# Second attention layer: turned probabilities by sixteen SBUF-to-SBUF transfers a tile in place of a way through DRAM

## The chip, the cores and the metric

The kernel runs on one core of a Trainium2 chip, in fp32 (the attention mask is added in bf16). The metric is the device time of one execution in microseconds (us). Five engines work side by side: PE (TensorE, matmuls; PEld is its loading of weights), DVE (VectorE), ACT (ScalarE), POOL (GpSimd) and SP (SyncE). In this kernel SP does nothing but issue DMAs. Sixteen DMA engines move the data.

## The reference

x has the shape [8, 512, 512] (8 batches of 512 tokens), ctx [8, 120, 512] (120 keys a batch). Four sublayers are added to x one after the other, each on a layer norm of x:

```python
x = x + tanh(g_xattn[0]) * L0_xattn(layernorm(x), ctx, ctx, Wq, Wk, Wv, Wo)
x = x + tanh(g_ffn[0])   * L0_ffn(layernorm(x), Wc, bc, W1, b1, W2, b2)
x = x + tanh(g_xattn[1]) * L1_xattn(layernorm(x), ctx, ctx, key_mask, Wq, bq, Wk, bk, Wv, bv, Wo, bo)
x = x + tanh(g_ffn[1])   * L1_ffn(layernorm(x), W_r, W_k, W_v, mu_r, mu_k)

# attention, both layers (mask and biases in the second alone); H = 16 heads of 32
q, k, v = split_heads(Q @ Wq.T), split_heads(K @ Wk.T), split_heads(V @ Wv.T)
scores = einsum('bhqd,bhkd->bhqk', q, k) / sqrt(32)
probs = softmax(scores)                         # [8, 16, 512, 120]
out = einsum('bhqk,bhkd->bhqd', probs, v) @ Wo.T
```

The change is in the second attention layer. The product of the probabilities with v sums over the keys, so PE needs the probabilities with keys on the partitions, while the softmax leaves them with tokens on the partitions: they have to be turned. L1_ffn is called ChannelMix in the kernel; it mixes each token with the one before it and multiplies with three 512 x 512 weights (W_k, W_r, W_v).

## The kernel before

x stays in SBUF, as 32 tiles of 128 tokens (NT = 32), 4 tiles a batch (TB = 4). The stages follow one another: attention 1 (0 to some 420 us in the profile), routed FFN (to 625), attention 2 (628 to 1040), ChannelMix (to the end). The order of the work is written out by hand: the instructions of each engine run in the order of the program (`tc.manual_schedule`), and waits between engines are semaphores.

**A step of the attention.** `steady(k)` (the last function below) works on four tiles at once, for k from 4 to 27:
- scores of tile k on PE (L656 adds the mask, L666 multiplies: 32 matmuls), into PSUM in two halves; a half comes free when tile k's exponentials have read it;
- softmax of tile k: the maximum of each half on DVE (L710, `nmx`), 32 exponentials on ACT with their sums (L721), 1/sum on DVE (L727) and the division on POOL (L731), in two halves u = 1 and u = 0;
- the turn of tile k's second half and tile k-1's first half on DVE (L793);
- the output product of tile k-3 (L878) and its addition to x (L888);
- products for the next batch's queries (L165, seven products for four tiles, by the scheme of seven in place of eight; three of four steps hold two products, the step with k % 4 = 3 holds one);
- the transposing of normalized x of tile k+8 (L588), the product of probabilities and v of tile k-2 (`attend`, L861), and the normalization of tile k+9.

**How probabilities are turned.** For the 22 tiles in `CROSSED` (4 to 25 of each layer) PE isn't used for it. The softmax writes a tile's probabilities as [128 tokens, 16 heads, 4 x 32 places], where key 4f + k stands at place f of piece k; 30 of 32 places hold keys and two hold zeros. DVE transposes blocks of 32 x 32 in place (L793). Then the 32 keys of a block are on partitions, but of four token groups q on four groups of partitions. Two DMAs a tile write the tile to a plane in DRAM (L796, 512 KB for each half), and four DMAs read it back (L806, 240 KB each), for piece k the 30 rows of each token group, to every fourth partition of `prT`:

```python
# turn_blocks, L796                       # fetch_blocks, L806
plane[:, :, u, :] <- pr half u            prT[k:120:4] <- plane[k, :30]     # for k in 0..3
```

In `steady(k)` the plane's last half (tile k-1, u = 0) is written near the start, behind the maxima; the fetch of tile k-1 is issued at the end, behind `attend(k-2)`, because `prT` has one buffer. `attend(k-1)` reads it at the end of `steady(k+1)`. All DMAs of this stage are issued by SP. The probabilities themselves (`pr`) have two buffers in the pool `soft`; the zeros in each are written once, and for the crossed tiles the same two buffers are handed on (the list `wide`).

`self.turned` (L236) is true in the second layer alone.

**ChannelMix beside it.** In the second layer `self.then` is a method of ChannelMix, which starts its own first work within the attention. `start` (L1396 and on) is called in the first slots: it takes the pool `cm_w` and loads `mu` (8 DMAs, L1406) and the weights wk and wr (4 DMAs of 256 KB each, L1415). wk is first read by POOL at 992.84 us (L91), wr near 1043 us, both in ChannelMix's preparations.

Of the kernel before, what the change touches and what calls it, by code (L numbers as in the profile page):

```python
# [9 lines left out]
FP = mybir.dt.float32  # L10
# [7 lines left out]
P = 128  # L18
B, S, D = 8, 512, 512
LK = 120  # L20
NH, HD = 16, 32
NT = B * S // P
TB = S // P
NC = D // P
# [8 lines left out]
KB, KF = 4, 30  # L33
CROSSED = range(TB, NT - TB - 2)
# [186 lines left out]
class CrossAttention:  # L221
# [455 lines left out]
    def softmax(self, t, sv):  # L677

        nc, soft = self.nc, self.soft
        if t - 2 in CROSSED and t in CROSSED:
            whole = self.wide.pop(0)
        else:
            whole = soft.tile([P, NC * S], FP, name="pr")
            if t in CROSSED:
                rows = whole.rearrange("p (n f) -> p n f", f=32)  # L690
                nc.gpsimd.memset(rows[:, :, KF:], 0.0)
        if t in CROSSED:
            self.wide.append(whole)
        sm = soft.tile([P, 2, 2, NC], FP, name="sm")
        rs = soft.tile([P, 2, 2, NC], FP, name="rs")
        nmx = [soft.tile([P, 2, NC, 1], FP, name=f"nmx{u}") for u in range(2)]
        self.probs[t] = whole
        crossed = t in CROSSED
        if crossed:
            half = [  # L700
                whole[:, u * 1024 : (u + 1) * 1024].rearrange(
                    "p (k h f) -> p k h f", k=KB, h=2 * NC
                )[:, :, :, :KF]
                for u in range(2)
            ]
        else:
            half = whole[:, : NH * LK].rearrange("p (u h k) -> p u h k", u=2, k=LK)

        def largest(u):
            nc.vector.tensor_reduce(nmx[u], sv[u], AX.X, ALU.max, negate=True)  # L710

        def exponentials(u, heads=range(2 * NC)):
            for h in heads:
                j, hc = divmod(h, NC)
                src = sv[u][:, j, hc, :]
                if crossed:
                    dst = half[u][:, :, h, :].rearrange("p k f -> p f k")
                    src = src.rearrange("p (f k) -> p f k", k=KB)
                else:
                    dst = half[:, u, h, :]  # L720
                nc.scalar.activation(  # L721
                    dst, src, AF.Exp, bias=nmx[u][:, j, hc, :],
                    accum_out=sm[:, u, j, hc : hc + 1],
                )

        def divide(u):
            nc.vector.reciprocal(rs[:, u], sm[:, u])  # L727
            by = rs[:, u].rearrange("p j h -> p (j h)")
            if crossed:
                by = by.unsqueeze(1).unsqueeze(3).to_broadcast([P, KB, 2 * NC, KF])  # L730
                nc.gpsimd.tensor_tensor(half[u], half[u], by, ALU.mult)  # L731
            else:
                by = by.unsqueeze(2).to_broadcast([P, 2 * NC, LK])
                nc.gpsimd.tensor_tensor(half[:, u], half[:, u], by, ALU.mult)

        return largest, exponentials, divide
# [52 lines left out]
    def turn_blocks(self, t, u):  # L789

        nc = self.nc
        pr = self.probs[t][:, u * 1024 : (u + 1) * 1024]
        nc.vector.transpose(pr, pr)  # L793
        if u == 1:
            self.planes[t] = self.dram.tile([KB, P, 2, 256], FP, name="plane")
        nc.sync.dma_start(  # L796
            out=self.planes[t][:, :, u, :].rearrange("k p e -> p k e"),
            in_=pr.rearrange("p (k e) -> p k e", k=KB),
        )

    def fetch_blocks(self, t):

# [125 lines left out]
    def steady(self, k):  # L928

        b, f = divmod(k + TB, TB)  # L930
        crossed = k in CROSSED
        if k == TB:
            self.transpose_probs_late(k - 1)
        largest, exponentials, divide = self.softmax(k, self.score_products(k))
        for u in (1, 0):
            largest(u)
        if k - 1 in CROSSED:
            self.turn_blocks(k - 1, 0)
        done = {TB: TB - 2, TB + 1: None}.get(k, k - 3)
        if done is not None:  # L940
            self.output(done, range(2 if done == TB - 1 else 0, NC))
        exponentials(1)
        divide(1)
        if done is not None:
            self.after(done, "final")
        exponentials(0, range(4))
        if f == 0:
            self.begin_queries(b)
        self.q7.postponed = True
        self.q7.next()  # L950
        exponentials(0, range(4, 8))
        if crossed:
            self.turn_blocks(k, 1)
        self.q7.settle(1)
        divide(0)
        if f != TB - 1:
            self.q7.next()
        if f == 0:
            self.sum_tokens(2)
        self.q7.settle()  # L960
        self.after(k, "route")
        if k + 8 < NT:
            self.transpose_x(k + 8)
        if k == TB:
            self.attend(k - 1)
        elif k == TB + 1:
            self.output(TB - 1, range(2))
        else:
            self.attend(k - 2)
        if k - 1 in CROSSED:  # L970
            self.fetch_blocks(k - 1)
        if k + 9 < NT:
            self.normalize(k + 9)
        if done is not None:
            self.after(done, "late")
# [403 lines left out]
class ChannelMix:  # L1379
# [16 lines left out]
    def start(self):  # L1396
        nc = self.nc
        wr_in, wk_in, wv_in, mu_in = self.ins
        self.pool = pool = self.es.enter_context(
            self.tc.tile_pool(name="cm_w", bufs=1, side="right", reuse_waits="tile")  # L1400
        )
        self.mu = pool.tile([P, 2, NC], FP, name="mu")
        for m in range(2):
            by_row = mu_in[:, m, :].rearrange("(j e) q -> q e j", j=NC)
            for q in range(4):
                nc.sync.dma_start(out=self.mu[32 * q : 32 * q + 32, m, :], in_=by_row[q])  # L1406
        self.om = pool.tile([P, 2, NC], FP, name="om")
        self.wk = self.load_rows(pool.tile([P, NC, D], FP, name="wk"), wk_in)
        self.wr = self.load_rows(pool.tile([P, NC, D], FP, name="wr"), wr_in)

    def load_rows(self, w, w_in):

# [33 lines left out]
    def in_slot(self, s, attention, stage):  # L1446

        nc = self.nc
        self.at = attention
        if stage == 2 and s >= 1:  # L1450
            attention.stats(s - 1)
        if stage == "final" and s < NT - 2 * TB:
            attention.stats(s, False)
        if stage == "late" and s < NT - 2 * TB:
            attention.scales(s)
        if s == -1:
            self.start()
        if stage == "head" and s == NT:
            self.sum_value_weights()
            self.k7.next()  # L1460
        if stage == "end" and s < NT:
            self.normalize(s - NT + 2 * TB)
        if stage == "end" and s == NT + 1:
            for c in range(NC):
                self.mix_chunk(0, 0, c)
            self.k7.next()
        if stage == "end" and s == NT + 2:
            for step in self.sum_steps(0, 0):
                step()
            self.k7.next(2)  # L1470
            self.sum_gate_weights()
        if stage != "route":
            return
        if s == TB + 1:
            nc.vector.tensor_scalar(self.om, self.mu, -1.0, 1.0, ALU.mult, ALU.add)
        i = s - (NT - 9)
        if 0 <= i - 1 < TB:
            self.transpose(i - 1)
        if 0 <= i < TB:
            xn = self.at.norm.tile([P, D], FP, name="xn")  # L1480
            self.normalize(i, xn)
        if s == NT - 4:
            wv = self.at.pool.tile([P, NC, D], FP, name="wv", tag="wq")
            self.wv = self.load(wv, self.ins[2])
            self.weight_sums = self.sum_key_weights()
        if 0 <= s - (NT - 5) < NC:
            self.mix_chunk(0, 1, s - (NT - 5))
        if s in (NT - 4, NT - 3):
            for _ in range(2):
                self.weight_sums.pop(0)()  # L1490
        if s == NT - 2:
            self.key_sums = self.sum_steps(0, 1, nc.gpsimd)
        if s in (NT - 2, NT - 1):
            for _ in range(2):
                self.key_sums.pop(0)()
        if s == NT - 1:
            self.k7 = self.keys(0)
            self.k7.next()
        if s in (NT, NT + 1):
            self.k7.next()  # L1500
# [385 lines left out]
```

## Time and profile before

| | |
|---|---|
| median of three runs | 1345.24 us (1342.72, 1345.24, 1347.89) |
| the profiled execution | 1344.26 us, its span 1342.4 us |
| granted PE clock | 0.996 |
| PE busy | 1283.4 us, 96% of the span |
| DVE, ACT, POOL busy | 75%, 59%, 53% |
| DMA queue of SP | 173.43 MB, 41.3% of 16 engines |
| plane written (L796) | 88 DMAs of 512 KB, landing 3.4 us after issue |
| prT fetched (L806) | 176 DMAs of 240 KB, landing 4.1 us after issue |

The profiled execution lies 1.0 us under the median and 1.9 us above its own span. A row of a group gives the line, engine, operation, tiles (out<-in) and count; in a row of a line's DMAs, the three numbers are minimum, median and maximum of one issue in ns. "SPq" is SP's issuing of DMAs, which the profile doesn't count as busy time. A timeline row gives start, duration, engine, line and operation, and in brackets the idle time ahead of it and what ended it. A wait for several semaphores is put down to the one that came last by the profile.

### The profile page before, as it was taken

What the parts mean: (1) busy time and instruction counts of PE and PEld (TensorE: products, weight loads), DVE (VectorE), ACT (ScalarE), POOL (GpSimd) and SP (SyncE); (2) the same over time, 40 slices, a digit from 0 to 9 for tenths busy, and PEclk for the clock granted to TensorE, in tenths of its full rate; (3) what the DMA queues carried; (4) which work ended last, traced back from release to release, by engine and by line L of the source; (5) the groups of instructions that cost most, each with busy time, mean ns of one, the idle gap of its engine ahead of it and who ended that gap; (6) DMA issues with size and microseconds to landing.
All of it is one profiled execution on the core that took longest, in us unless ns stands there. A gap on an engine that the chain in (4) does not pass through costs nothing. (4 is left out here: it accounts for less than half of the span.)

```text
span 1342.4 us, 32798 instructions
## 1 busy us (share of the span) xinstructions
PE 1283.4 (96%) x13072; PEld 1014.9 (76%) x13072; DVE 1001.5 (75%) x1476; ACT 791.4 (59%) x2512; POOL 705.2 (53%) x626
## 2 busy tenths in 40 slices
PE   7999999999999988999999989999999999999997
PEld 6886777777776877888888767676766888878886
DVE  5877776777685676777888687777775977878876
ACT  1368788888774445455226778888874454444442
POOL 4855655565542002555797777777665234434333
PEclk9999999999999999999999999999999999999999
DMA  9501766666603256431402067767621211333201
GB/s 308 194 1 62 225 208 205 222 211 214 195 26 110 75 168 212 127 112 63 155 12 54 32 205 222 216 211 226 213 81 33 63 67 60 94 94 94 63 32 63
DMA packets 136382, 175.53 MB, mean 131 GB/s; under 512 B 9197, under 2 KB 88557, under 8 KB 136229
## 3 DMA queue, kind: packets, MB, share of 16 engines
q1 hardware_dynamic: 136229, 173.43, 41.3%
q8 instruction: 103, 1.69, 0.5%
q14 instruction: 50, 0.41, 0.1%
HBM read 101.18 MB, written 72.22 MB: 129 GB/s over the span
## 5 line engine op out<-in xcount | busy, mean ns | idle before, releaser
L721 ACT ACTIVATE pr<-s,nmx 128x120 f32<-128x120 f32 x768 | 273.5, 497 | 43.1 <-DVE nmx L710 24.8
L878 PE MATMUL ops<-wo,aT 128*128 128x512 f32 x512 | 237.0, 604 | 3.6 <-ACT aT L869 2.2
L731 POOL TENSOR_TENSOR pr<-pr,rs 128x960 f32<-128x960 f32 x88 | 160.2, 1820 | 139.0 <-DVE rs L727 137.2
L721 ACT ACTIVATION_READ_ACCUMULATOR pr<-s,nmx 128x1 f32 x768 | 195.0, 254 | 0.0
L878 PEld LDWEIGHTS ops<-wo,aT 128*128 128x128 f32 x512 | 91.9, 189 | 99.8 <-issue 89.1
L1353 POOL TENSOR_TENSOR r<-r,b 128x1024 f32<-128x1024 f32 x31 | 73.5, 2377 | 147.8 <-ACT r L1352 147.8
L710 DVE TENSOR_REDUCE nmx<-s 128x8 f32<-128x960 f32 x96 | 106.7, 1153 | 56.9 <-PE s L666 56.8
L793 DVE STREAM_TRANSPOSE pr<-pr 128x1024 f32<-128x1024 f32 x88 | 109.1, 1240 | 37.3 <-POOL pr L731 37.3
L165 PE MATMUL qps<-xnT,wq 128*128 128x256 f32 x512 | 119.0, 380 | 0.0
L165 PEld LDWEIGHTS qps<-xnT,wq 128*128 128x128 f32 x512 | 96.3, 189 | 23.3 <-issue 10.3
L52 DVE BATCH_NORM_STATS2 bnst<-x 128x6 f32<-128x512 f32 x128 | 87.6, 684 | 0.4
L1629 ACT ACTIVATE kT<-kT 128x512 f32<-128x512 f32 x32 | 19.9, 622 | 108.1 <-DVE kT L183 59.6
L759 POOL TENSOR_TENSOR pr<-pr,rs 128x960 f32<-128x960 f32 x32 | 58.1, 1823 | 40.8 <-DVE rs L758 31.5
L861 PE MATMUL aps<-prT,v 120*32 120x128 f32 x2048 | 69.2, 276 | 7.7 <-DVE qT L212 3.3
L888 DVE SCALAR_TENSOR_TENSOR x<-ops,gates,x 128x512 f32<-128x512 f32 x64 | 47.7, 746 | 34.6 <-PE ops L878 34.1
L666 PE MATMUL s<-kT,qT 32*128 32x120 f32 x2048 | 71.6, 275 | 0.0
L666 PEld LDWEIGHTS s<-kT,qT 32*128 32x128 f32 x2048 | 65.7, 186 | 7.0 <-issue 4.9
L861 PEld LDWEIGHTS aps<-prT,v 120*32 120x32 f32 x2048 | 52.2, 109 | 21.3 <-issue 8.6
L1352 ACT COPY r<-rps 128x1024 f32<-128x1024 f32 x31 | 31.4, 1013 | 59.1 <-PE rps L1340 59.1
L1340 PE MATMUL rps<-ident,rT 128*128 128x128 f32 x512 | 61.9, 275 | 2.1 <-DVE rT L1320 1.8
L1350 DVE TENSOR_TENSOR r<-rps,b 128x1024 f32<-128x1024 f32 x33 | 40.4, 1225 | 28.3 <-PE rps L1340 28.3
L1340 PEld LDWEIGHTS rps<-ident,rT 128*128 128x128 f32 x512 | 55.5, 141 | 7.7 <-issue 4.8
(240 smaller groups left out, 3092.1 us busy)
## 6 DMA issues: line engine op xcount, KB each, us to landing
plane<-pr SPq DMA_DIRECT2D x88, 512.0 KB, 3.4
prT<-plane SPq DMA_DIRECT2D x176, 240.0 KB, 4.1
w<-in_w_dram SPq DMA_DIRECT2D x32, 512.0 KB, 4.4
x<-in_x_dram SPq DMA_DIRECT2D x8, 1024.0 KB, 16.8
aside<-x SPq DMA_DIRECT2D x32, 256.0 KB, 3.0
x<-aside SPq DMA_DIRECT2D x8, 1024.0 KB, 10.2
rows<-xn SPq DMA_DIRECT2D x14, 512.0 KB, 2.8
xn<-rows SPq DMA_DIRECT2D x56, 128.0 KB, 3.2
```

Of the source, the lines that this page charges most:

```text
L52: cm.nc.vector.bn_stats(st, cm.x[:, t, :])
L165: self.nc.tensor.matmul(ps[:, m, :], rows[:, k, m * n : (m + 1) * n], columns[:, k, :], start=(k == 0), stop=(k == 1),)
L666: nc.tensor.matmul(s[j // 2][:, j % 2, hc * LK : (hc + 1) * LK], self.qT[b][r : r + 32, hc, toks], self.kT[r : r + 32, hc, keys], start=no ...
L710: nc.vector.tensor_reduce(nmx[u], sv[u], AX.X, ALU.max, negate=True)
L721: nc.scalar.activation(dst, src, AF.Exp, bias=nmx[u][:, j, hc, :], accum_out=sm[:, u, j, hc : hc + 1],)
L731: nc.gpsimd.tensor_tensor(half[u], half[u], by, ALU.mult)
L759: nc.gpsimd.tensor_tensor(pr[:, js, :, :], pr[:, js, :, :], rs[:, js, :, :].to_broadcast([P, 2, NC, LK]), ALU.mult,)
L793: nc.vector.transpose(pr, pr)
L861: nc.tensor.matmul(out, self.v[b // 2][:LK, b % 2, h * HD : (h + 1) * HD], p, start=True, stop=True,)
L878: nc.tensor.matmul(ops, self.aT[t][:, c, :], self.wo[:, c, :], start=(c == 0), stop=(c == NC - 1),)
L1340: nc.tensor.transpose(ps[:, k // 4, (k % 4) * P : (k % 4 + 1) * P], self.rT[:, 16 * tq + 8 * h + k, :], self.cm.ident,)
L1353: nc.gpsimd.tensor_tensor(r, r, b2, ALU.add)
```

## The change

In the second layer only:
- the probabilities of a tile are laid out piece by piece, "(k u e)" in place of "(u k e)": the 512 values of piece k lie side by side on a partition, and a half u is four pieces of 256 (`half_of`);
- the plane in DRAM goes. `move_blocks(k-1)`, called in `steady(k)` right behind `turn_blocks(k-1, 0)`, issues 16 DMAs from SP, for each token group q and piece k one: 32 partitions x 512 values (64 KB), from 32 neighbouring partitions of `pr` to every fourth partition of `prT`;
- `prT` gets a second buffer for odd tiles ("prT2", in the place of ChannelMix's wr) and `pr` a third one ("pr2", in the place of wk, first used by tile 4);
- the loads of wk and wr move from ChannelMix's start to the steps s = 26 and s = 30 of the attention (NT - 6, NT - 2).

The order of PE's and ACT's instructions stays. On DVE the 44 transposes of the layer read and write 128 x 4 x 256 in place of 128 x 1024, on POOL its divisions get one more dimension and one memset of zeros is added. SP issues 352 DMAs for the 22 tiles, where it issued 132.

```diff
@@ softmax
-        if t - 2 in CROSSED and t in CROSSED:
+        bufs = 3 if self.turned else 2
+        if t - bufs in CROSSED and t in CROSSED:
             whole = self.wide.pop(0)
         else:
-            whole = soft.tile([P, NC * S], FP, name="pr")
+            if self.turned and t == CROSSED[0]:
+                whole = self.then.__self__.place("pr2", "wk")
+            else:
+                whole = soft.tile([P, NC * S], FP, name="pr")
...
             half = [
-                whole[:, u * 1024 : (u + 1) * 1024].rearrange(
-                    "p (k h f) -> p k h f", k=KB, h=2 * NC
-                )[:, :, :, :KF]
+                self.half_of(whole, u).rearrange("p k (h f) -> p k h f", h=2 * NC)[:, :, :, :KF]
                 for u in range(2)
             ]
@@ turn_blocks
-        pr = self.probs[t][:, u * 1024 : (u + 1) * 1024]
+        pr = self.half_of(self.probs[t], u)
         nc.vector.transpose(pr, pr)
+        if self.turned:
+            return
...
+    def half_of(self, whole, u):
+        if self.turned:
+            halves = whole.rearrange("p (k u e) -> p u k e", k=KB, u=2)
+        else:
+            halves = whole.rearrange("p (u k e) -> p u k e", k=KB, u=2)
+        return halves[:, u]
+
+    def move_blocks(self, t):
+        if t % 2:
+            prT = self.then.__self__.place("prT2", "wr")
+            prT = prT.rearrange("p (q e) -> p q e", q=4)
+        else:
+            prT = self.late.tile([P, 4, 512], FP, name="prT", bufs=1)
+        blocks = self.probs.pop(t).rearrange("p (k e) -> p k e", k=KB)
+        for q in range(4):
+            for k in range(KB):
+                self.nc.sync.dma_start(
+                    out=prT[k::KB, q], in_=blocks[32 * q : 32 * q + 32, k]
+                )
+        self.probs[t] = prT
@@ steady
         if k - 1 in CROSSED:
             self.turn_blocks(k - 1, 0)
+            if self.turned:
+                self.move_blocks(k - 1)
...
-        if k - 1 in CROSSED:
+        if k - 1 in CROSSED and not self.turned:
             self.fetch_blocks(k - 1)
@@ ChannelMix.start
-        self.wk = self.load_rows(pool.tile([P, NC, D], FP, name="wk"), wk_in)
-        self.wr = self.load_rows(pool.tile([P, NC, D], FP, name="wr"), wr_in)
+
+    def place(self, name, tag):
+        return self.pool.tile([P, NC * S], FP, name=name, tag=tag)
@@ ChannelMix, called by the attention at each step s
+        if s == NT - 6:
+            wk = self.pool.tile([P, NC, D], FP, name="wk")
+            self.wk = self.load_rows(wk, self.ins[1])
+        if s == NT - 2:
+            wr = self.pool.tile([P, NC, D], FP, name="wr")
+            self.wr = self.load_rows(wr, self.ins[0])
```

More of the change, by code (lines that the diff above doesn't have):

```diff
@@ L797, in turn_blocks @@
             out=self.planes[t][:, :, u, :].rearrange("k p e -> p k e"),
-            in_=pr.rearrange("p (k e) -> p k e", k=KB),
+            in_=pr,
         )
+    def half_of(self, whole, u):
[17 more added lines that the diff above has]
+        self.probs[t] = prT
     def fetch_blocks(self, t):
```

## The prediction

> **What bounds the kernel now.** I read the page first (which engine is busy where), then a table by stretches of the second layer's steady part, then what TensorE waited for there, then single waits in the timeline, and last the rows of the DMAs by line. The table by stretches of the steady part (us; then busy time and instructions of PE, PEld, DVE, ACT, POOL; clock; DMA share; GB/s):
>
> ```profile
> 780.00:860.00 80.00, 77.44 (x825) 54.27 (x823) 60.95 (x92) 66.24 (x307) 60.55 (x47) 1.00 0.73 219
> 860.00:940.00 80.00, 79.51 (x774) 54.75 (x768) 61.83 (x90) 65.58 (x307) 60.24 (x52) 1.00 0.72 219
> 940.00:980.00 40.00, 38.56 (x387) 26.80 (x389) 27.07 (x41) 32.86 (x158) 24.60 (x20) 1.00 0.71 218
> ```
>
> PE is busy for 195.5 of 200 us: the stage runs at PE's pace, and the DMA engines, at 0.71 to 0.73, wait for nobody else. All that is left to win is in the other 4.5 us. The waits of PE between 780 and 980, and the three places where prT stands behind them:
>
> ```profile
> PE aps L861 <- DMA prT<-plane: 2.5, 2, 1.6
> PE aps L861 <- PE xnps L588: 1.5, 4, 0.8
> PE ops L878 <- ACT aT L869: 0.4, 1, 0.4
> ...
> 782.19 1.08 PE L861 MATMUL aps<-prT,v 120*32 120x128 f32 x32 [1.56 <-DMA prT<-plane]
> ...
> 866.19 1.08 PE L861 MATMUL aps<-prT,v 120*32 120x128 f32 x32 [0.28 <-PE xnps L588]
> ...
> 979.94 1.08 PE L861 MATMUL aps<-prT,v 120*32 120x128 f32 x32 [0.93 <-DMA prT<-plane]
> ```
>
> The reader is to see that the turned probabilities are late for a few tiles only. The second kind of line names PE itself, which had long been done; the last prT transfer landed 0.13 to 0.23 us ahead of each of these starts, and 0.5 to 1.6 us ahead in all other tiles. So prT stands behind 2.5 + 1.5 = 4.0 us, and no more than that can be won.
>
> **What the change takes out.** For 22 tiles the plane in DRAM goes, with 2 + 4 transfers a tile. Of the 4.0 us not all comes back, because the next scores wait for PSUM that ACT's exponentials free, and these end shortly before. Tile by tile, that slack (next scores' start less the end of the last exponential) is 0.35 us behind 782.19, 0.60 behind 791.09, and -0.1 to 0.0 in the four short slots (828, 866, 904, 941), which PE enters after some 8.3 us in place of 9.73. At 979.94, DVE's next maximum has 0.2 us. That gives about 0.5 + 0.75 + 4 x 0.1 + 0.2 = **-1.9 us**, if the new transfers are in time. The third buffer of probabilities gains nothing by itself: the exponentials start 0.22 to 0.24 us after the maximum (nmx) that they read, so no buffer held them.
>
> **What it adds.** 16 transfers a tile from SP's queue, 352 in all, where 132 were. Each carries 32 rows of 2 KB, from 32 neighbouring partitions to every fourth partition of prT. They are issued one after the other from the moment of the first half's turn (now the plane write, 769.55 for tile 4 and 966.97 for tile 25). The whole question is what one issue costs SP. These are the rows (duration of an issue, ns min/median/max; in the timeline: start, us, instructions):
>
> ```profile
> L806 SPq DMA_DIRECT2D prT<-plane x176: 822/838/1635, 133.3 to 974.7; - x176
> ...
> L796 SPq DMA_DIRECT2D plane<-pr x88: 359/365/556, 123.8 to 967.0; - x88
> ...
> L1406 SPq DMA_DIRECT2D mu<-in_mu_dram x8: 345/430/433, 687.5 to 690.7; - x8
> ...
> L1415 SPq DMA_DIRECT2D wk<-in_wk_dram x4: 312/430/1101, 702.4 to 703.7; - x4
> ...
> L303 SPq DMA_DIRECT2D ctxT<-turned x2: 561/584/607, 627.8 to 653.8; - x2
> ...
> L327 SPq DMA_DIRECT2D bv<-in_bv_dram x1: 578/578/578, 654.5 to 654.5; - x1
> ...
> 687.46 3.67 SPq L1406 DMA_DIRECT2D mu<-in_mu_dram  x8
> ...
> 784.13 3.48 SPq L806 DMA_DIRECT2D prT<-plane  x4
> ```
>
> Eight issues of mu take 3.67 us, four of prT 3.48. Bytes do not explain it: mu carries 512 bytes in a transfer, wk 256 KB, and both cost 430 ns behind one another (345 and 312 alone). Next to wk, the fetch of prT has two peculiarities: 30 rows in place of 32, and a destination that steps over four partitions. The new transfers lose the first and keep the second. So the two ends are:
> - **430 ns**, the price of 32 rows to neighbouring partitions (wk, mu);
> - **823 ns**, that of the fetch as it stands, if the step is all of it.
>
> Between them I split by the rows whose counts aren't round but that have no step. ctxT (1920 bytes a row) took 561 ns after SP had idled, against 346 for bqk in the same place: +215. bv (120 rows) took 578 behind another, against 438 for gbo (128 rows): +140. Taking these from prT's 840 (after idling) and 823 (behind one another) leaves 840 - 215 = 625 and 823 - 140 = 683 for a stepped transfer with round counts. I take **625 ns**: the fetch is the only row with the same destination and the same step, and the odd count explains at most half of what it costs above wk. With the 45 ns between two issues (wk's and mu's starts lie 475 apart) the pitch is p = 0.67 us.
>
> Time on SP: 16 x 0.67 = 10.7 us a tile, where PE has a tile every 9.37 us (three slots of 9.73 and one of 8.3). Now SP is the bound, from the first moved tile on. The last transfer of tile 25 is issued 351 p after the first of tile 4. It lands about 2.4 us later: mu (512 bytes) lands after 1.7, rows of 128 KB (xn<-rows) after 3.2, and a move of 64 KB is between them; 0.2 us more till PE starts. 769.55 + 351 x 0.67 + 2.6 = 1007.3, against 979.94 now: **+27.4 us**. That PE is held up doesn't hold up SP in turn: from a landing over attend (1.1), the next scores (1.2), two maxima (2.3) and a transpose (1.2) to the next tile's first move are some 6 to 8 us, and the moves of the tile between take 10.7.
>
> What depends on this bound: with pitch p, SP is in time as long as 769.55 + 351 p + 2.6 stays under 979.0 (the present start less its wait of 0.93), so up to **p = 0.59**, an issue of 0.545 us. Above that every 0.1 us costs 35 us. A single tile on a free SP is done after 15 p + 2.6, at 0.475 after 9.7 us, and has 11.1 (tiles 4, 5) to 12 us.
>
> [...] The rows show that a transfer of 512 bytes and one of 256 KB hold SP for the same 430 ns. [...]
>
> **The small terms, taken at nothing.**
> - DVE's transposes read and write four pieces of 256 in place of 1024 in a row (1240 ns each); DVE waits for scores 23.7 us in 21 tiles, 1.1 a tile, which covers up to 0.5 us on each. Bounds: 0 and, uncovered, 0.1 us a tile, 2 us.
> - POOL's division gets one more dimension; 1820 ns with 32 x 30 and 1823 with 8 x 120 show no cost of shape. Bounds 0 and 2 us.
> - PE waits for eight queue positions in place of four before attend, 51 ns each on its sequencer; PE takes such waits 0.5 to 3 us ahead of the matmul. Bounds 0 and 22 x 4 x 0.051 = 4.5 us.
> - The loads of ChannelMix's wk and wr move from 702 to behind tile 25's moves. POOL reads wk at 992.84; on a free SP the moves are issued by 975 and wk lands by about 985, some 8 us ahead. On a late SP both ends shift alike. If the cover were gone, the key weights would be late by what is missing. wr is needed near 1043. Nobody waited for them at 702.
> - One more memset, of padding, lies ahead of the steady part.
>
> **Rivals.**
> - **A transfer that is in time (ends on the other side).** An issue costs 430 to 545 ns, SP needs 7.6 us of 9.37 at 0.475, and only the 1.9 us are left: 1344.3 - 1.9 = **1342.4**. For it: every 32-row row shows 430, and odd counts do raise the price. Against: they raise it by 140 to 215, and the fetch is 393 above. It decides from an issue under 0.545.
> - **The step is all.** 823 ns, p = 0.868: 769.55 + 304.7 + 2.6 = 1076.9, +96.9: **1441**. For: the same destination. Against: the odd rows above.
> - **It doesn't do what it says**: SP isn't held by issuing but by the eight queue positions, each free when its transfer has landed. Eight moves per landing: over 4.6 us they bind. At prT's slowest landing of 5.4, 2 x 5.5 = 11 us a tile, +1.6 x 21 = **+34**, 1378. Against: the traffic of a tile halves, and smaller transfers landed in 1.7 to 3.2.
> - **Faster by over 0.5%** needs 6.7 us; the waits hold 4.0. Only a cause that the profile doesn't show.
>
> **How the numbers follow.** The profiled execution took 1344.26 us (span 1342.4), 1 us under the median of 1345.24. Forecast: 1344.3 + 27.4 = 1371.7, **1372 us**, its own range 1354 to 1390 (p from 0.62 to 0.72: +9.9 to +45). Chances: forecast 0.42, in time 0.34, step alone 0.13, landings 0.07, faster 0.04. The range takes in both ends of the issue cost and the raw waits: 1340 (-4.0) to 1441. A measurement of this kernel can tell some 0.5% from no change: faster 0.04, same 0.34, slower 0.62.
>
> **What would show it.** The duration of the move's issue is the first thing to read: 0.625 with starts 0.67 apart, and SP without idle time from 770 to 1005; aps waits for prT's DMA in nearly every tile, some 1.3 us each, and the slots grow from 9.37 to 10.7. An issue of 430 ns, with SP idle for 1.8 us a tile and the six waits at aps gone, would make the forecast wrong and the first rival right. Landings over 4.6 us with SP waiting between issues would show the third. If POOL or DVE stand before PE instead, a small term was wrong.

## The result, and the profile after

| | before | after |
|---|---|---|
| median | 1344.49 us (4 runs, 1342.72 to 1347.89) | 1375.25 us (4 runs, 1374.31 to 1376.63) |
| ratio, 95% interval | | 1.0234 (1.0212 to 1.0257) |
| span of the profiled execution | 1342.4 us | 1373.8 us |

The changed kernel is slower by 30.8 us; 1372 was forecast. The table by stretches of the second layer's steady part, now to 1000 us (us; then busy time and instructions of PE, PEld, DVE, ACT, POOL; clock; DMA share; GB/s):

```profile
780.00:860.00 80.00, 69.83 (x704) 49.04 (x706) 54.69 (x82) 59.14 (x278) 54.59 (x43) 0.98 0.38 100
860.00:940.00 80.00, 73.44 (x703) 49.88 (x702) 54.33 (x78) 58.24 (x268) 52.19 (x42) 0.96 0.38 99
940.00:1000.00 60.00, 54.01 (x543) 38.55 (x545) 38.84 (x60) 43.59 (x200) 34.51 (x27) 0.97 0.39 100
```

All compute engines are less busy than before, and the DMA engines' share has halved (0.38 from 0.72). Nothing that the profile counts as busy is a bound here. What PE waits for between 770 and 1020 us (in total, times, longest):

```profile
PE aps L888 <- DMA prT<-pr: 26.1, 17, 3.5
PE s L656 <- ACT pr L723: 1.4, 1, 1.4
```

So it is the turned probabilities. Their issues by SP, as a line's row (ns min/median/max) and in the timeline (start, us):

```profile
L823 SPq DMA_DIRECT2D prT<-pr x352: 470/592/1755, 771.0 to 1007.3; - x176
...
DMA to landing us min/median/max: 2.0/2.1/3.9
```

```profile
770.99 29.10 SPq L823 DMA_DIRECT2D prT<-pr  x44
```

One issue takes 592 ns, the next starts 637 ns after it, and SP issues without a break: the timeline draws 44 moves as one block of 29.1 us. Sixteen of them are over 10 us of SP's time, where PE had a tile every 9.37 us. The landing, 2.1 us, is not late; each move lands soon after its issue. The steps k = 6 to 26 now take 9.7 to 12.9 us, most of them 10.2 to 11.3; from tile 4's matmul on the probabilities to tile 25's they average 10.8, where 10.7 was forecast.

### The profile page after: what moved, and what is told of

Its sections match the earlier page's. It is cut to its first block, busy times and chain, and to the rows that moved or that the text cites. A ratio compares the mean times of both kernels' runs of the same rounds, so it can differ in the third digit from the quotient of the medians.

```text
span 1373.8 us, 33149 instructions
## 1 busy us (share of the span) xinstructions
PE 1292.2 (94%) x13072; PEld 1020.5 (74%) x13072; DVE 1001.9 (73%) x1476; ACT 791.9 (58%) x2512; POOL 704.5 (51%) x627
## 4 chain that ended last, share of the span: by engine, by line
PE 56%; DVE 17%; SPq 7%; POOL 7%; ACT 6%; issue 5%; DMA 2%; ACTq 0%; DVEq 0%; POOLq 0%
PE ops L905 13%; PE qps L165 10%; SPq L823 7%; PE cps L165 4%; PE s L666 4%; PE aps L888 4%; PE rps L1369 3%; PE vps L165 2%; PE l1ps L1284 2%; PE ops L1390 2%; PE gps L1257 2%; DVE rT L1349 2%; DMA prT<-pr 2%; PE rlps L1103 2%; PE kps L165 1%
## 5 line engine op out<-in xcount | busy, mean ns | idle before, releaser
L905 PE MATMUL ops<-wo,aT 128*128 128x512 f32 x512 | 240.7, 612 | 3.2 <-ACT aT L896 1.9
L733 POOL TENSOR_TENSOR pr<-pr,rs 128x960 f32<-128x960 f32 x88 | 159.7, 1815 | 161.2 <-DVE rs L729 151.6
L795 DVE STREAM_TRANSPOSE pr<-pr 128x1024 f32<-128x1024 f32 x88 | 109.1, 1240 | 35.5 <-POOL pr L733 32.3
L1381 ACT COPY r<-rps 128x1024 f32<-128x1024 f32 x31 | 31.4, 1013 | 59.1 <-PE rps L1369 59.1
L896 ACT COPY aT<-aps 128x512 f32<-128x512 f32 x64 | 37.7, 589 | 42.5 <-PE aps L888 42.5
```

The source lines that it names most:

```text
L905: nc.tensor.matmul(ops, self.aT[t][:, c, :], self.wo[:, c, :], start=(c == 0), stop=(c == NC - 1),)
```

## The experiments

Each is the changed kernel with an edit, where nothing else is said; times are medians, ratios go against the kernel before on the same chip.

**Half the bytes, half the moves.** Is SP bound by the number of issues, or by what they carry?

```diff
-                    out=prT[k::KB, q], in_=blocks[32 * q : 32 * q + 32, k]
+                    out=prT[k::KB, q, :256], in_=blocks[32 * q : 32 * q + 32, k, :256]   # e4_half_bytes
```

> The changed kernel, except that each of the 16 moves carries 256 of the 512 values of a row, and heads 8 to 15 are given the probabilities of heads 0 to 7: half of the moving is left out. Theory 'SP is bound by the number of issues': issue 592 ns, time about 1375 as before it. Rival 'bytes or landings hold it': the issue or the landing gets shorter and the time falls towards 1358 or less.

1376.1 us (one run, span 1374.3), and the row of the moves:

```profile
L823 SPq DMA_DIRECT2D prT<-pr x352: 469/592/1812, 770.0 to 1008.1; - x176
```

The issue takes 592 ns as with all bytes: here a move of 32 KB and one of 64 KB cost SP the same.

```diff
-        for q in range(4):
+        for q in range(2):           # e5_eight; attend reads groups 0 and 1 twice
```

> The changed kernel, except that only 8 of the 16 moves of a tile are made (token groups 0 and 1) and attend gives token groups 2 and 3 the probabilities of 0 and 1: half of the moving is left out. Theory 'SP is bound by the number of issues': 8 x 0.67 = 5.4 us a tile, SP idle for 4 us of 9.37, prT in time everywhere, and the time 1342.4 (before less the 1.9 us that the waits for prT allow). Rival 'another part of the change costs too' (the transposes' or division's form, PE's waits, the late weights): the time stays above before.

1343.24 us, ratio 0.997 (0.9959 to 0.9982): with eight moves a tile the whole loss is gone, and 4.0 us (2.4 to 5.5) are won. What PE waits for in this run between 770 and 1020:

```profile
PE s L656 <- ACT pr L723: 2.2, 2, 1.4
PE ops L908 <- ACT aT L899: 0.4, 1, 0.4
PE tps L867 <- ACT aT L899: 0.4, 2, 0.2
```

No wait for prT is left. The other parts of the change (the layout, the buffers, the weights' later loads, PE's longer waits) are all in this run, so together they cost less than what prT in time brings.

**Two moves more.** The same theory upward: two issues added to each tile.

```diff
+        spare = self.late.tile([P, 256], FP, name="spare", bufs=2)
+        for n in range(2):
+            self.nc.sync.dma_start(
+                out=spare[n::KB], in_=blocks[32 * n : 32 * n + 32, n, :256]
+            )
```

> The changed kernel with two more moves a tile, behind the sixteen: two of the blocks (256 values of a row) go once more, to a spare tile that nobody reads; nothing is left out. Theory 'SP is bound by the number of issues': 22 x 2 x 0.637 = 28 us more than the changed kernel, so about 59 us over before, a ratio of 1.044. Rival 'something else of the change holds the stage, and SP merely fills the time': the time stays near the changed kernel's, 1.023.

1402.67 us, ratio 1.0437 (1.0413 to 1.0460): 57.5 us over before, 26.8 us more than the changed kernel's 30.8. 44 issues at 0.637 are 28.0, and one still takes 592 ns. From sixteen to eighteen moves the time goes as the number of issues says; with eight, SP has room and PE sets the pace.

**Is it the step over partitions?** This was the prediction's reason for the price.

```diff
-                    out=prT[k::KB, q], in_=blocks[32 * q : 32 * q + 32, k]
+                    out=prT[32 * k : 32 * k + 32, q], in_=blocks[32 * q : 32 * q + 32, k]
```

> The changed kernel, except that piece k goes to 32 neighbouring partitions of prT (32k to 32k+31) in place of every fourth one, so attend meets the keys in another order than v has them and the end of piece 3 isn't read: a part of the computation is changed, the work is the same. Theory 'step' (the destination's step of four partitions is what lifts an issue from 430 ns to the 592 measured): the issue falls to about 430 ns, SP needs 16 x 0.475 = 7.6 us a tile plus its stalls, PE sets the pace again and the time is about 1342. Rival 'SBUF to SBUF' (the price comes from both ends being in SBUF, or from 64 KB transfers as such): the issue stays at 592 ns and the time at about 1375.

```profile
L823 SPq DMA_DIRECT2D prT<-pr x352: 507/589/1868, 770.3 to 1007.7; - x176
```

1377.18 us, ratio 1.0227 (1.0210 to 1.0244), the issue 589 ns: without the step it costs the same. My theory falls here: the price of a move doesn't come from the step.

**And the fetch's 30 rows?** The kernel before, with all 32 rows fetched in the second layer:

```diff
-            self.nc.sync.dma_start(out=prT[k:LK:KB], in_=plane[k, :KF])
+            if self.turned:
+                self.nc.sync.dma_start(out=prT[k::KB], in_=plane[k])
+            else:
+                self.nc.sync.dma_start(out=prT[k:LK:KB], in_=plane[k, :KF])
```

> The kernel before, except that in the second layer each fetch from the plane takes all 32 rows of a piece (two of them zeros) and not 30; the step of four partitions stays. The first layer is left at 30 rows beside it. The prediction's split (823 = 430 + 140 to 215 for the odd count + the rest for the step): an issue of 610 to 690 ns in the second layer, 823 in the first. Rival 'the step is all of it': 823 in both. Rival 'the odd count is all of it': 430 in the second. The time stays within 2 us of before in each case, since SP is not the bound there.

The two layers' rows in this kernel (L807 is the second layer, 32 rows; L809 the first, 30):

```profile
L807 SPq DMA_DIRECT2D prT<-plane x88: 582/600/1952, 775.6 to 978.2; - x88
L809 SPq DMA_DIRECT2D prT<-plane x88: 822/834/1647, 134.1 to 364.7; - x88
```

32 rows cost 600, 30 rows 834 (time 1348.1, one run; the kernel before had a median of 1347.5 on this chip). So a transfer from DRAM with the step costs what a move from SBUF costs with or without it. Neither kernel has all forms side by side.

**The forms by themselves.** A kernel of issues alone, each line eight transfers of 2 KB rows, twice:

```diff
+        for j in range(8):
+            nc.sync.dma_start(out=d[32:64, j], in_=near[0:32, j])         # L43: SBUF to SBUF
+            nc.sync.dma_start(out=d[j % 4 :: 4, j], in_=far[j, 0:32])     # L40: from DRAM, step 4
+            ...                                                           # and so on
```

> A kernel that computes nothing of the reference: it issues eight transfers of 2 KB rows behind one another in each of 14 forms, twice, into tiles that nothing else touches (source in DRAM or in SBUF; 16, 30, 32, 64 or 128 rows; destination to neighbouring partitions or every fourth; one store to DRAM; one form from ACT's and one from POOL's queue), so that the price of an issue is seen without the attention beside it. Theory 'either peculiarity lifts the price once' (SBUF as source, or a destination step, each takes a 32-row issue from 430 to about 592 to 600, and both together no further; an odd count adds about 230): DRAM 32 rows 430, with the step 600, SBUF to SBUF 590 with and without the step, 30 rows with the step 823. Rival 'the stage sets the price' (the same transfers are dearer in the attention than elsewhere): all 32-row forms cost 430 here. Rival 'rows set it': the price goes with the number of rows, whatever the ends are.

The rows in the order: from DRAM 32 rows, from DRAM with the step, SBUF to SBUF, SBUF to SBUF with the step, from DRAM 30 rows, the same with the step, SBUF to SBUF 30 rows, 16 rows, 128 rows, and the store to DRAM:

```profile
L37 SPq DMA_DIRECT2D to<-far x16: 302/421/1226, 15.9 to 172.2; - x16
L40 SPq DMA_DIRECT2D to<-far x16: 487/592/595, 28.1 to 183.0; - x16
L43 SPq DMA_DIRECT2D to<-near x16: 560/590/597, 39.5 to 194.1; - x16
L46 SPq DMA_DIRECT2D to<-near x16: 500/594/595, 50.4 to 205.0; - x16
L49 SPq DMA_DIRECT2D to<-far x16: 314/403/407, 61.4 to 215.0; - x16
L52 SPq DMA_DIRECT2D to<-far x16: 768/769/890, 70.7 to 227.2; - x16
L55 SPq DMA_DIRECT2D to<-near x16: 778/779/806, 83.8 to 239.9; - x16
L58 SPq DMA_DIRECT2D to<-near x16: 558/589/590, 96.2 to 251.0; - x16
L64 SPq DMA_DIRECT2D to<-near x16: 484/610/617, 118.3 to 273.1; - x16
L71 SPq DMA_DIRECT2D there<-near x16: 322/422/579, 21.5 to 293.5; - x16
```

Read as pairs: the step lifts a load from DRAM from some 420 to 592 ns; a move from SBUF to SBUF costs as much without it (590), and both together no more (594). 30 rows cost nothing on the cheap form (403 against 421) and 180 to 190 on the dear one (769, 779). The other row counts in these lines hardly matter: 16 take as long as 32 (589 against 590), and 128 only 20 ns more (610). The prices of 32 rows are those of the attention with no attention beside them, so the rival "the stage sets the price" falls for them. It doesn't for 30 rows with the step: 823 were expected and 769 came, where the fetch, with four pieces of 2 KB a row, takes 834. What inside SP or behind it makes the two classes isn't shown.

**The second buffer of prT alone, the way through DRAM kept** (the kernel before, fetching 32 rows right behind the plane's last write):

```diff
             self.turn_blocks(k - 1, 0)
+            if self.turned:
+                self.fetch_blocks(k - 1)
...
-        if k - 1 in CROSSED:
+        if k - 1 in CROSSED and not self.turned:
             self.fetch_blocks(k - 1)
```

> The kernel before with the change's second buffer of prT alone: the way through DRAM stays, and in the second layer the four fetches of a tile are issued right behind the plane's last write, near the start of a step, and take all 32 rows; the load of wr moves to step 30. SP needs 2 x 0.4 + 4 x 0.65 us a tile and 3.4 us of waiting for the plane, some 7 of 9.37 us, and prT is there about 6 us after the plane's write, 5 us ahead of its use. Theory 'the only gain in the change is prT in time, the sixteen issues are its only loss': prT waits vanish, time -2 to -4 us from before, like the run with eight moves. Rival 'the second buffer or the late weights cost something': same as before or slower.

1353.77 us, ratio 1.0052 (1.0034 to 1.0069): slower by 7 us, and the expectation missed. Its waits, and SP's timeline over two tiles:

```profile
PE aps L868 <- DMA prT<-plane: 9.9, 5, 2.5
```

```profile
825.53 2.53 SPq L811 DMA_DIRECT2D prT<-plane  x4
828.15 1.09 SPq L796 DMA_DIRECT2D plane<-pr  x2
836.01 2.53 SPq L811 DMA_DIRECT2D prT<-plane  x4
838.64 1.09 SPq L796 DMA_DIRECT2D plane<-pr  x2
```

The fetch can't start before the plane has landed, and while it waits in SP's queue, the next tile's first half is held behind it: SP issues nothing from 829.24 to 836.01 us. Both halves of that tile are then written right behind one another (the second starts 0.64 us after the first, in the median; before, 5.4), and land after a median of 6.0 us in place of 3.7 (785 to 975 us in both). So the fetch, meant to be earlier, is later: it starts 6.6 us behind its plane's last write, where it started 5.1 us behind it before. What an added wait has queued behind it was the term that I left out.

**Some of the moves from POOL.** If SP is short, can another queue take a quarter? Two to four of the sixteen moves by `nc.gpsimd.dma_start`, right behind the turn or behind POOL's last division of the step:

```diff
-                self.nc.sync.dma_start(
+                (self.nc.gpsimd if q == 3 else self.nc.sync).dma_start(      # e8; e9: q == 3 and k > 0
...
         divide(0)
+        self.move_rest()              # e10, e11 (k > 0), e13 (k > 1): q == 3 from POOL here
```

> The changed kernel, except that the four moves of token group 3 are issued by POOL and only twelve by SP; nothing is left out. Theory 'the sixteen issues on SP are the whole loss': SP needs 12 x 0.637 + 0.6 (instruction fetches beside them) = 8.2 us of 9.37 a tile, PE sets the pace, and the time is that of the run with eight moves, 3 to 5 us under before, if POOL can give 4 x 0.50 = 2.0 us a tile out of the 2.5 it has idle. Rival 'POOL takes SP's place': its moves wait for DVE's turn with POOL's division queued behind them, the divisions come late by up to 2 us a tile, and of the change's 30 us some remain.

1374.81 us, ratio 1.0225 (1.0209 to 1.0241).

> As the run before it, with three moves from POOL and thirteen from SP: SP needs 13 x 0.637 + 0.6 = 8.9 us of 9.37, POOL gives 1.5 us. The theory says the same time as with four; if POOL's share is what costs, it is less than with four; if SP's share is, more.

1363.83 us, ratio 1.0146 (1.0129 to 1.0163).

> As the run with four moves from POOL, but POOL issues them behind its last division of the step, where nothing waits for it until the next step's first division some 5 us later; nothing is left out. If the place in POOL's order was what cost there (a division 2.15 us late in each tile), the time falls from 1.0225 of before to 0.997 to 1.000, the time of the run with eight moves: SP needs 8.2 us of 9.37 a tile. If POOL's total load is what costs (167 of 200 us busy), the time stays over 1.01.

1366.19 us, ratio 1.0148 (1.0127 to 1.0169).

> The same with three moves from POOL, thirteen from SP: 8.9 us on SP of 9.37, 1.6 on POOL. Expected as the run with four, 0.997 to 1.000 of before; if SP is what is short there, it lies above that run, if POOL is, below it.

1355.02 us, ratio 1.0059 (1.0043 to 1.0075).

> As the run with three late moves from POOL, with two, fourteen from SP; nothing is left out. SP needs 14 x 0.637 + 0.6 = 9.5 us of 9.37, some 3 us too much over 22 tiles, and POOL gives 1.1 us a tile. By the steps so far (four late moves on POOL 1.0148, three 1.0059) the loss on POOL should be nearly gone: a ratio of 0.998 to 1.003. If it isn't, a POOL-issued move costs more than the time it takes to issue.

1350.40 us, ratio 1.0032 (1.0019 to 1.0045).

None of them beats before. The first of the two fences shows the run with four early moves, POOL's timeline in one step; the second DVE's waits in the run with three late ones, 780 to 980 us:

```profile
815.10 2.15 POOL L823 DMA_DIRECT2D prT<-pr  x4
817.27 1.82 POOL L733 TENSOR_TENSOR pr<-pr,rs 128x960 f32<-128x960 f32 x1
```

```profile
DVE pr L795 <- DMA prT<-pr: 28.2, 9, 4.0
DVE pr L795 <- POOL pr L733: 23.6, 11, 4.0
```

The same row before, where no other names L793:

```profile
DVE pr L793 <- POOL pr L731: 16.0, 20, 1.6
```

In the run with four early moves POOL's issues take 2.15 us (538 ns each), and the division starts when they are over. PE then waits for the exponentials behind it, 17.4 us between 775 and 1000 us, where no such wait lies in before. In the run with three late moves DVE's transposes wait 51.8 us in all, against 16.0. Nine of these twenty waits are named after a DMA, yet each of the twenty ends 34 or 35 ns behind the end of a division on POOL, as before's twenty do (32 to 34 ns): it is POOL that they wait for. Issuing later in POOL's order costs less (1.0148 in place of 1.0225 with four moves, 1.0059 in place of 1.0146 with three), but POOL is busy for 165 to 174 of 200 us in the late runs, against 145, and each move taken off POOL gains some 3 to 11 us. SP's shortage has moved to POOL; with two moves left on POOL, SP is short again and idles for only 3.6 us between its first move and its last.

## Why the prediction was right, step by step

- **The mechanism held.** SP's queue is the bound from the first moved tile on, PE waits for prT in most tiles, and the stage's pace is SP's. The signs that the prediction named came out: SP has no idle time, PE waits 1.5 us for prT in 17 of the 22 tiles (1.3 in nearly every tile were forecast), the steps grow to 10.8 us. Only the size of the issue is off: 592 ns for 625, starts 637 apart for 670.
- **The sum came out by two errors that cancel, which is luck.** 351 x 0.637 = 223.6 us, not 235.2. Yet the last move starts 236.3 us after the first (771.0 to 1007.3), a mean pitch of 0.673. 17 of the 20 issues over 0.7 us (up to 1755 ns) lie beside a packet of the instruction queue; the 20 exceed 592 ns by 12.2 us in all. In the window of these moves the page of the DMA queues shows these packets, 16 KB each:

```profile
q1 hardware_dynamic: 16808, 22.98, 37.3%
q8 instruction: 17, 0.28, 0.5%
```

  Each of the 17 packets (0.9 to 1.6 us by the trace's records) overlaps a lengthened issue, also in the runs without the step and with half the bytes (17 of 17 in each); with eight moves, where SP sits idle for some 90 of 200 us, 3 of 16 do. That they hold SP's issue is inferred from this; no run took the packets away. The same rows stand in before, as 14 prT issues over 1000 ns, and I read over them: it was the term missing from the sum.
- **The account.** From the first move to PE's first matmul on tile 25's probabilities: 223.6 + 12.2 + 0.5 (single gaps) + 2.6 (landing and start, as forecast) = 238.9 us, against 210.4 from the same two points before: +28.5, forecast +27.4. The remaining 2.9 us of the spans' 31.4 lie outside it: the second layer's moves start 1.4 later, and the rest of the kernel takes 1.5 longer.
- **The reason for the price was wrong.** I took the 823 ns of the fetch for 430 + an odd count (140 to 215) + the step. The odd count was estimated from ctxT and bv; by themselves, 30 rows to neighbouring partitions cost nothing extra (403 ns against 421). From DRAM the step costs 160 to 190 and the odd count some 180 on top of it (234 in the fetch itself, 600 to 834), and a move pays the first of these already without a step, as a transfer from SBUF to SBUF. That 625 lies near 592 is partly luck: with neighbouring partitions the prediction would have said 430 and 1342, and the run gave 1377.
- **The first rival** (an issue of 430, 1342.4) failed by its price alone. What it promised is there when SP has room: 1343.24 with eight moves, 4.0 us (2.4 to 5.5) under before where 1.9 were worked out. In the two traces 2.6 us of this lie in the stage, from PE's matmul on tile 3's probabilities to that on tile 25's (213.6 us in place of 216.2): 1.1 by tile 6, where 0.5 + 0.75 were worked out, 0.5 over the four short slots and those behind them (4 x 0.1), and 1.0 at tile 25, where DVE's next maximum was taken to leave 0.2. So the slack that I subtracted held but for the last tile. Where the rest of the 4.0 comes from, if it isn't scatter, isn't shown.
- **The second and third**: "the step is all" (823, 1441) is excluded by the row. Landings were 2.1 us, far from the 4.6 at which, by the prediction's reckoning, the eight positions bind. In after's trace SP's DMAs go through eight semaphores in turn, and each move starts 1.9 us or more after the last DMA on its semaphore has landed.
- **The small terms** taken at nothing cost less together than prT in time brings, since the run with eight moves has them all and is faster than before: DVE's transposes take 1240 ns in both, POOL's divisions 1815 against 1820.

## What to carry to other kernels

Count the DMAs that a queue issues per step, multiply by the time from one issue's start to the next, and hold it against the step's time, also where the DMA engines are half idle (busy for 0.38 of the time here): 16 x 0.67 us stood against 9.37. Take the price of an issue from a row with the same ends, for here it went with where source and destination are and not with bytes (430 ns at 512 bytes and at 256 KB, 592 at 32 KB and at 64 KB), and measure the form by itself if no row has both. Before a quarter of the issues goes to another engine, or a wait into the queue, name what stands behind it there: both attempts here lost for that.

## What the runs showed of the hardware that was not expected

- Two classes of issue on SP among the forms measured alone: 403 to 432 ns in the median between DRAM and neighbouring partitions, either way, and 589 to 610 where both ends are in SBUF or the destination steps over partitions; 30 rows add 180 to 190 (769 and 779 ns) in the second class and nothing in the first (403). Rows of before that fit neither: ctxT (561, 607) and bv (578), and the loads of x, 1 MB each, with issues of up to 5.2 us. What lifts these wasn't tested. From ACT's queue the SBUF-to-SBUF form took 610 ns, from POOL 496 (538 in the attention), as busy time of POOL.
- Single issues are lengthened to 0.9 to 1.8 us beside a 16 KB packet of the instruction queue (17 of 17 in the stage), 12 us in all where SP sets the pace.
- In the stage in which PE waits, its granted clock fell to half for 3.4 or 6.8 us at a time, four times after (at 836.7, 881.0, 966.4 and 1010.8 us; none before in this stage). Each follows an idle time of PE, of 2.3, 2.1, 2.3 and 3.5 us; others of 2.1 to 2.2 us (793.9, 922.9) were followed by none. In the trace's clock records three of the falls last 3.412 to 3.413 us and the one at 881.0 lasts 6.827. The four falls are 44.4, 85.3 and 44.4 us apart, which is 13, 25 and 13 times 3.413 us, and in windows of that length that end at the falls PE is idle for 2.1 to 2.5 us ahead of each fall and for at most 1.6 us in every other window from 770 to 1015 us. The idle times of 793.9 and 922.9 lie across the border of two windows. Counted so in four more runs (without the step, half the bytes, eighteen moves, the early fetch), all 18 windows with over 1.9 us of idle time end in a fall, and below that only three do, near 775 to 778 us with 1.4. PE is busy for 1292.2 us after, 1283.4 before. A wait in after's timeline, and two stretches around it, the second with PE at half speed and no idle time:

```profile
880.16 1.14 PE L888 MATMUL aps<-prT,v 120*32 120x128 f32 x32 [2.13 <-DMA prT<-pr]
```

```profile
876.00:880.00 4.00, 2.03 (x12) 1.55 (x10) 3.55 (x7) 3.63 (x21) 1.82 (x1) 1.00 0.40 101
...
884.00:888.00 4.00, 4.00 (x6) 1.47 (x5) 2.97 (x3) 3.08 (x19) 1.54 (x2) 0.52 0.38 101
```

  With eighteen moves, where PE waits longer, the same is seen more often (mean clock 0.976 against 0.990 after). Here it costs little, since SP goes on issuing meanwhile: behind the one long step of 12.9 us two follow of 9.7 and 9.8 without a wait for prT. No run was made to test whether it is idle time in such windows that makes the clock fall, and the three falls after 1.4 us are not explained.
